# First slots of 128 token-expert pairs for every expert, gathered ahead, and the first batch's scores ahead of the third batch's work

## The chip, the cores and the metric

The kernel runs as one program on one core of a Trainium2 chip. The metric is the device time of one execution in microseconds (us), as the median of several runs; lower is better. Profiles come from one further execution on the same kind of core. PE is the matmul engine, DVE the vector engine, ACT the scalar engine, POOL the general-purpose engine that also issues the indirect DMAs (gathers and scatters by a list of row numbers), SP the engine that issues most plain DMAs.

## What is computed

Two layers on x of shape (8, 256, 512), float32: 2048 tokens, 16 tiles of 128. The reference, cut to what matters here:

```python
def _L0_cond_ref(x, Wq, Wk, Wv, Wo, ..., k_blocks, v_blocks, block_tables, kv_lens):
    ...                       # projections, RMS norm, rotation, paged K/V cache
    p = softmax(where(allowed, qg @ k_all.T * SCALE, -inf))   # window of 256 keys
    return (p @ v_all) @ Wo.T

def _L0_ffn_ref(x, gate_w, W, atoms, expert_atom_weights, importance, mask_idx):
    logits = clip(xt @ gate_w.T, -50, 50)
    top_w, top_idx = top_k(logits, 2);  rw = softmax(top_w)
    weighted = (softmax(expert_atom_weights) @ atoms) * sigmoid(importance)
    ...                       # out = xt @ W.T + sum over 2 experts of
    return out                # rw * (sparse change of W by expert) applied to xt

def _L1_cond_ref(x, W, A, Bm, scalings, adapter_idx):
    return x @ W.T + (x @ A[idx].T @ Bm[idx].T) * scalings[idx]     # per batch

def _L1_ffn_ref(x, gate_w, fc1_w, fc1_b, fc2_w, fc2_b, alpha):
    probs = softmax(x @ gate_w);  gate_score, gate_idx = top_k(probs, 2)
    h = gelu(x @ fc1_w[e] + fc1_b[e]);  y = h @ fc2_w[e] + fc2_b[e]
    return sum over the 2 experts of gate_score/sum * alpha[e] * y

x = x + _L0_ffn_ref(_L0_cond_ref(x, ...), ...)
x = x + _L1_ffn_ref(_L1_cond_ref(x, ...), ...)
```

Each token goes to two of eight experts in each layer, so each layer has 4096 token-expert pairs.

## The kernel before

The work runs in stages, one after the other; the times are those of the profile.

**Projection and keys (0 to about 115 us)** make keys, values and the sparse weight changes, which are added into delta_d in DRAM, one 512x512 weight per expert.

**Attention (115 to 400 us)** takes eight batches in a loop. Batch b first gathers old and new key and value rows for batch b+2 (`find_rows`, `gather_old`, `gather_new`, POOL's indirect DMAs), projects batch b+2's queries on PE (`queries`, L1098) and has DVE normalise and rotate them, and then does `attend` for its own two tiles of 128 tokens: scores ps on PE (L1420), mask and maximum on DVE (L1435), exp on ACT (L1451), sum and scale on DVE, transposes pp (L1465), their copies pT on ACT (L1469), and the product po (L1474), copied to oT (L1484). Between the two tiles `prepared` transposes the keys of batch b+1 (pk L1390, KT L1393). After them `gate_rows` makes the routing logits lg0 of the batch, and `output_rows` (L635) multiplies by Wo and writes rows to h_d in DRAM: tiles 0 to 8 (`EARLY = 9`) inside this loop, the other seven after it. po, pk, pq, pg, pt and the early ph share two PSUM banks under the tag "misc" of the pool ps_o. `start_sums` fills the sums in DRAM from x and zeros.

**Routing of layer 0 (400 to 437 us).** `top2` (cmp L468/L475, sel L482/L483), `shifted_exp` and `normalized` (L498 to L500) choose two experts per token on DVE for all 16 tiles at once, while POOL and ACT re-arrange half of delta (L623). `route` ranks every pair within its expert (`ranks`: pst L215, pn L219, prk L222/L223) and turns ranks into slots by a `Plan`. A *slot* is a group of 128 pairs that is gathered, multiplied and scattered together. `Plan` has two kinds: *full* slots, 128 pairs of one expert fixed in advance, and *paired* slots, two halves of 64 pairs: one half's expert is fixed (`side`), the other's is found at run time (`owner_i`). Layer 0 has 8 full and 26 paired slots, layer 1 has 22 full and 12 paired. `fill_slots` makes the list: one-hot matrices hot (L312) and put (L293 to L305) on DVE, 64 matmul records pm (L319) on PE, giving for each slot 128 row numbers (token_i) and 128 weights (L329). Pairs that find no slot would be handled in a branch (`run_rest`, L1752) that is not entered for these inputs. Between the pm matmuls and beside the last output rows, `fold_adapters` (L1586, L1635, L1646) prepares layer 1's low-rank adapters.

**Slots of layer 0 (437 to 586 us).** For each slot `fetched` (L533) gathers 128 rows of h_d by an indirect DMA, `turned` transposes them (pa L569, copy xsT L575), `multiplied` does the product (full slots L547 with 8 matmuls of 128x512; paired slots L556 with 16 matmuls, each over 64 columns, two abreast), ACT scales by the weight (L1794) and `added` (L580) scatters with addition into one of two sums in DRAM. Gathers run three slots ahead, transposes two. At L1726/L1732, layer 1's fc1 weights (8 MB) and half of fc2 (4 MB) are loaded by SP as soon as their place is free.

**Boundary and layer 1's projection (586 to 684 us).** `fold_gate` (pga L1665) finishes the adapter weights; the two sums are read back (part, L1838) and added to x1; for four groups of four tiles (`quads`; a quad holds one tile of each of four batches) `turn`, `inner` (px L1852) and `outer` (pc L1876, L1887) compute the layer's linear part and adapters; ACT copies each tile to g (L1895) and writes it to g_d (L1896), 16 writes. The order of the quads is not the order of the tiles, and g_d is laid out by tile. The routing of layer 1 runs on DVE and PE beside `outer`. The second half of fc2 is loaded behind the part reads and the writes of x1 to out, fc2's bias (L1937) after the last outer.

**Slots of layer 1 (695 to 968 us).** As in layer 0, with fc1 (pu L1978), gelu (L2004), fc2 (L547 or L556), bias and weight on DVE (L2020, L2021), and the scatter into out (L580).

The order of instructions on each engine is set by a scheduler (with estimates of cost) except where `keep_in_program_order` or `in_a_row` fix it. A gather waits for every write to the DRAM rows that its source names: in both layers the whole of h_d or g_d.

Of the kernel before, what the change touches and what calls it, by code (L numbers as in the profile page):

```python
# [19 lines left out]
P = 128  # L20
# [32 lines left out]
class Plan:  # L53
# [5 lines left out]

    PAIRED, FULL = 128 * HR, 256 * HR  # L60

    def __init__(self, full, side):
        self.full = [e for e in range(E) for _ in range(full[e])]
        self.side = [e for e in range(E) for _ in range(side[e])]
        self.F, self.D = len(self.full), len(self.side)
        self.n = self.F + self.D
        self.by_expert = []
        for e in range(E):
            t = HR * side[e]
            u = t + P * full[e]  # L70
            second = self.PAIRED + HR * (self.F + sum(side[:e]))
            whole = self.FULL + P * sum(full[:e]) - t
            first = HR * self.F - u
            self.by_expert.append((t, u, second + 1, whole - second, first - whole))


PLAN0 = Plan([1] * E, [3] * 6 + [4] * 2)
PLAN1 = Plan([3] * 6 + [2] * 2, [1] * 6 + [3] * 2)
# [3 lines left out]
def two_layer_kernel(ctx: ExitStack, tc: tile.TileContext, io: dict, out: bass.AP):  # L82
# [9 lines left out]
    h_d = dram.tile([N + P, D], F32, name="h_d")  # L92


    g_d = dram.tile([N + P, D], F32, name="g_d")
# [47 lines left out]
    def routing_constants(pool, plan=None, late=False):  # L143
# [36 lines left out]
        nc.gpsimd.iota(tok_i, pattern=[[P, NT]], base=-N, channel_multiplier=1)  # L180
# [7 lines left out]
        if plan:  # L188
            fixed_i = pool.tile([P, 5, E], I32, name="fixed_i")
# [14 lines left out]
            fixed = pool.tile([P, 5, E], F32, name="fixed")  # L204
# [5 lines left out]
    def ranks(pool, psum, consts, sel):  # L210

        earlier, ahead, same_e = consts[:3]
        flat_sel = sel.rearrange("p i e -> p (i e)")
        pst = psum.tile([P, P], F32, name="pst", tag="route_a")
        nc.tensor.transpose(pst, flat_sel, ident)  # L215
        tot = pool.tile([P, 1], F32, name="tot")
        nc.vector.tensor_reduce(tot, pst, AX.X, ALU.add)
        pn = psum.tile([P, E], F32, name="pn", tag="route_a")
        nc.tensor.matmul(pn, tot.to_broadcast([P, P]), same_e, start=True, stop=True)  # L219
        prk = psum.tile([P, NT, E], F32, name="prk", tag="route_b")  # L220
        prk2 = prk.rearrange("p i e -> p (i e)")
        nc.tensor.matmul(prk2, earlier, flat_sel, start=True, stop=False)  # L222
        nc.tensor.matmul(prk2, tot.to_broadcast([P, P]), ahead, start=False, stop=True)  # L223
        return pn, prk
# [21 lines left out]
    def two_rows(pool, rows, cf, row, coef):  # L246
# [4 lines left out]
        at = pool.tile([P, NT, E], F32, name="at")  # L251
        nc.vector.tensor_tensor(
            at, row, rows[:, 1, :, None].to_broadcast([P, NT, E]), ALU.is_equal
# [20 lines left out]
    def fill_slots(keep, pool, psum, tag, consts, slot, rem, cf, n, at_once):  # L274
# [3 lines left out]
        what = pool.tile([P, 2, NT], F32, name="what")  # L278
        nc.vector.tensor_tensor(
            what,  # L280
            tok[:, None, :].to_broadcast([P, 2, NT]),
# [5 lines left out]
        pm = psum.tile([P, 2, n], F32, name="pm", tag="route_b")  # L287
        STEP = 4
        for j in range(0, 2 * NT, STEP):
            if j % at_once == 0:  # L290
                span = slice(j, j + at_once)
                put = pool.tile([P, at_once, 2, n], F32, name="put", tag="wide")
# [18 lines left out]
            hot = pool.tile([P, STEP, P], F32, name="hot", bufs=2)  # L311
# [6 lines left out]
            for k in range(STEP):  # L318
                nc.tensor.matmul(  # L319
                    pm.rearrange("p c s -> p (c s)"),  # L320
                    hot[:, k, :],
                    put[:, (j + k) % at_once].rearrange("p c s -> p (c s)"),
                    start=(j + k == 0),
                    stop=(j + k == 2 * NT - 1),
                )
        token_i = keep.tile([P, n], I32, name=f"token_i_{tag}")
# [3 lines left out]
        return token_i, weight  # L330

    def route(keep, pool, psum, consts, plan, sel, coef, tag, beside=None):
# [8 lines left out]
            boff, boff, float(HR), fixed[:, 4, :], ALU.mult, ALU.add  # L341
# [4 lines left out]
        for j, step in ((0, fixed[:, 3, :]), (1, boff)):  # L346
            past = row if j == 0 else far
            nc.vector.tensor_tensor(
                past, prk, fixed[:, j, None, :].to_broadcast(each), ALU.is_ge
            )  # L350
            nc.vector.tensor_tensor(
                past, past, step[:, None, :].to_broadcast(each), ALU.mult
            )
        nc.vector.tensor_tensor(row, row, far, ALU.add)
# [35 lines left out]
        )  # L390
        owner_i = keep.tile([P, plan.D], I32, name=f"owner_i_{tag}")
        find_owners(pool, owner_i, count, bend)

        if beside:
            beside()
        token_i, weight = fill_slots(
            keep, pool, psum, tag, consts, slot, rem, cf, plan.n, 2 * NT
# [9 lines left out]
        return token_i, weight, owner_i, left_i, (row, rows, left, coef)  # L407

    def route_rest(keep, pool, psum, places, used_i):

        row, rows, left, coef = places
        consts = routing_constants(pool)
# [3 lines left out]
        for r in range(2):  # L416
# [41 lines left out]
        token_i, weight = fill_slots(  # L458
            keep, pool, psum, "rest", consts, slot, rem, cf, NREST, 4
        )  # L460
        return token_i, weight, owner_i

    def top2(pool, val, tag):

        cmp = pool.tile([P, NT, E, E], F32, name=f"cmp_{tag}", tag="wide")
        for o in range(E):
# [3 lines left out]
                other.to_broadcast([P, NT, o + 1]),  # L470
# [3 lines left out]
            if o + 1 < E:  # L474
                nc.vector.tensor_tensor(  # L475
                    cmp[:, :, o + 1 : E, o],
                    other.to_broadcast([P, NT, E - 1 - o]),
                    val[:, :, o + 1 : E],
                    ALU.is_ge,
                )  # L480
        sel = pool.tile([P, NT, E], F32, name=f"sel_{tag}")
        nc.vector.tensor_reduce(sel, cmp, AX.X, ALU.add)  # L482
        nc.vector.tensor_scalar(sel, sel, 1.5, None, ALU.is_lt)  # L483
        return sel

    def shifted_exp(pool, val, tag):
        mx = pool.tile([P, NT], F32, name=f"mx_{tag}")
        nc.vector.tensor_reduce(mx, val, AX.X, ALU.max)
        ex = pool.tile([P, NT, E], F32, name=f"ex_{tag}")
        nc.vector.tensor_tensor(  # L490
            ex, val, mx[:, :, None].to_broadcast([P, NT, E]), ALU.subtract
        )
        nc.scalar.activation(ex, ex, AF.Exp)
        return ex

    def normalized(pool, val, tag):
        sm = pool.tile([P, NT], F32, name=f"sm_{tag}")
# [3 lines left out]
            val, val, sm[:, :, None].to_broadcast([P, NT, E]), ALU.mult  # L501
# [28 lines left out]
    def fetched(pool, rows_d, token_i, s):  # L530
# [6 lines left out]
            in_offset=bass.IndirectOffsetOnAxis(ap=token_i[:, s : s + 1], axis=0),  # L537
            bounds_check=N + P - 1,
# [39 lines left out]
    def added(sum_d, token_i, s, y):  # L578
# [3 lines left out]
            out_offset=bass.IndirectOffsetOnAxis(ap=token_i[:, s : s + 1], axis=0),  # L582
# [14 lines left out]
    delta = [dpool.tile([P, HK, E, D], F32, name="delta_0"), None]  # L597
    ost = ExitStack()
# [32 lines left out]
    def output_rows(i, psum, pool):  # L631

        ph = psum.tile([P, D], F32, name="ph", tag="misc")
# [13 lines left out]
    with ExitStack() as att:  # L647
# [79 lines left out]
        kcos = ap.tile([P, NT, HD], F32, name="kcos")  # L727
        ksin = ap.tile([P, NT, HD], F32, name="ksin")
# [247 lines left out]
        j_i = ap.tile([P, B, NCAND], I32, name="j_i")  # L976
# [21 lines left out]
        code_i = ap.tile([P, B, NCAND], I32, name="code_i")  # L998
# [149 lines left out]
        with proj:  # L1148
# [165 lines left out]
            for i in range(LEAD, NT):  # L1314
# [12 lines left out]
                if i in (6, 8, 10):  # L1327
                    find_rows(i // 2 - 3)
# [41 lines left out]
        sp = att.enter_context(tc.tile_pool(name="sp", bufs=4))  # L1370
        ps_s = att.enter_context(tc.tile_pool(name="ps_s", bufs=2, space=PSUM))
# [158 lines left out]

        beside = iter(())
        for b in range(B):
            kvs = kv_rows[b]
            if b + AHEAD < B:
                if b + AHEAD > 2:
                    find_rows(b + AHEAD)
                gather_old(b + AHEAD)
                gather_new(b + AHEAD)
# [4 lines left out]
            if b + 2 < B:  # L1543
                qrs = queries(b + 2)
# [5 lines left out]
            if b == 1:  # L1550
                for rest in (*sums_d, h_d, g_d):
                    nc.sync.dma_start(rest[N:, :], zero)
            attend(b, 0, kvs, QTs[b], *ready, beside)
            now = ready
# [13 lines left out]
            attend(b, 1, kvs, QTs[b], *now, beside)  # L1568
            gate_rows(b)
# [19 lines left out]
    def fold_adapters(keep, fold, psum):  # L1589
# [8 lines left out]

        an = keep.tile([P, D], F32, name="an")
        bn = fold.tile([P, KC, P], F32, name="bn")  # L1600
        other_side([aT[:, k, :] for k in range(KC)], an, psum)
        other_side(
            [bT[:, k * P : (k + 1) * P] for k in range(KC)], bn.rearrange("p c r -> p (c r)"), psum
        )
# [27 lines left out]
        nc.vector.tensor_scalar(scaled, pick, scal, None, ALU.mult)  # L1632
        for g in range(B // 4):
            pgb = psum.tile([P, D], F32, name="pgb", tag="misc")
# [9 lines left out]
        pbg = psum.tile([P, E], F32, name="pbg", tag="misc")  # L1644
# [46 lines left out]
    rp0 = dst_.enter_context(tc.tile_pool(name="rp0", bufs=1))  # L1691
    with ExitStack() as ffn:
# [435 lines left out]
```

## Time and profile before

| | us |
|---|---|
| Three runs | 976.61, 968.81, 968.16 |
| Median of the runs | 968.81 |
| The profiled execution's own time | 970.09 |
| Its span, from the first to the last instruction | 968.4 |
| PE busy in it | 901.9 |
| DVE busy in it | 455.5 |
| ACT busy in it | 371.8 |
| POOL busy in it | 360.3 |
| Last output row matmul of layer 0 ends | 426.8 |
| First slot gather of layer 0 issued, first slot transpose | 437.0, 442.3 |
| Last matmul of layer 1's projection ends | 684.1 |
| First slot gather of layer 1 issued, first slot transpose | 687.7, 695.3 |

The mean granted clock of PE is 0.979 of full speed. A row of the timeline gives the start, the duration, the engine (ACTq, SPq: an engine's queue issuing a DMA), the source line, the operation, what it writes and reads, its shape and type, a count where several in a row are put together, and in brackets the engine's idle time before it and what ended that. In a list of waits the numbers are the total, the times and the longest.

### The profile page before, as it was taken

The page shows a single profiled execution, that of the slowest core. Times are in us where ns is not written, and L with a number is a line of the kernel's source. Part 1 is how long each engine was busy: PE and PEld are TensorE (multiplying, and loading weights), DVE is VectorE, ACT ScalarE, POOL GpSimd, SP SyncE. Part 2 cuts the span into 40 slices and gives each one's busy share as a digit, 9 for nine tenths or more (in the row PEclk, how much of TensorE's full clock was granted, in tenths as well). Part 3 has the DMA queues.
Part 4 walks back from the last instruction along what each step waited for, and adds up shares of the span by engine and source line. Part 5 has one row for each costly group of instructions (what it writes and reads, how often), then busy time and mean ns, then how long its engine had stood idle before and what let it go on. Part 6 is the DMA issues. An engine that isn't in the chain of part 4 may idle for free. (4 is left out here: it accounts for less than half of the span.)

```text
span 968.4 us, 14307 instructions
## 1 busy us (share of the span) xinstructions
PE 901.9 (93%) x4829; PEld 491.8 (51%) x4829; DVE 455.5 (47%) x1487; ACT 371.8 (38%) x954; POOL 360.3 (37%) x335
## 2 busy tenths in 40 slices
PE   6998889999999997897999997999599999999995
PEld 3554445655555554464433333545377777753332
DVE  5788898846857766672211112470022223223332
ACT  3676475736647599631111113401111111122221
POOL 2721656557564200405666641000233333333211
PEclk9899999999999999997999999999799999999998
DMA  6587692342432212529997768961524443443322
GB/s 194 215 307 269 225 322 45 98 114 60 138 78 61 61 44 66 189 85 326 341 255 133 129 89 222 364 230 54 185 55 76 73 69 66 77 69 63 50 27 34
DMA packets 74237, 134.62 MB, mean 139 GB/s; under 512 B 17309, under 2 KB 22941, under 8 KB 74032
## 3 DMA queue, kind: packets, MB, share of 16 engines
q0 software_dynamic: 25088, 43.68, 24.2%
q1 hardware_dynamic: 38496, 74.57, 22.1%
q10 hardware_dynamic: 10576, 15.39, 4.3%
q8 instruction: 41, 0.67, 0.3%
q14 instruction: 36, 0.29, 0.1%
HBM read 89.95 MB, written 52.56 MB: 147 GB/s over the span
## 5 line engine op out<-in xcount | busy, mean ns | idle before, releaser
L533 POOL DMA_INDIRECT xs<-g_d,token_i_l x34 | 35.2, 1035 | 230.1 <-PE pa L569 129.5
L575 DVE COPY xsT<-pa 128x512 f32<-128x512 f32 x68 | 46.8, 688 | 155.1 <-PE pa L569 146.9
L2020 DVE TENSOR_TENSOR y<-py,b 64x512 f32<-64x512 f32 (+1 forms) x46 | 31.7, 690 | 185.9 <-PE py L547 122.2
L2004 ACT ACTIVATE hs<-pu,b 128x64 f32<-128x64 f32 (+1 forms) x184 | 46.0, 347 | 186.0 <-PE pu L1978 144.5
L1451 ACT ACTIVATE s<-s,mx,roots 128x384 f32<-128x384 f32 x128 | 90.0, 706 | 14.8 <-DVE mx L1447 10.7
L556 PE MATMUL py<-delta,xsT 128*64 128x512 f32 (+1 forms) x416 | 94.8, 598 | 0.0
L1978 PE MATMUL pu<-xsT,w 128*128 128x128 f32 x704 | 83.1, 277 | 0.0
L1978 PEld LDWEIGHTS pu<-xsT,w 128*128 128x128 f32 x704 | 81.1, 194 | 0.4 <-issue 0.4
L547 PE MATMUL py<-w,hs 128*128 128x512 f32 x176 | 79.3, 593 | 0.0
L1474 PE MATMUL po<-pT,kv 128*64 128x128 f32 x768 | 69.4, 285 | 6.4 <-ACT pT L1469 6.4
L580 POOL DMA_INDIRECT out<-y,token_i_l x34 | 53.9, 1584 | 55.8 <-DVE y L2021 51.3
L1159 PE MATMUL pkv<-wkv,xb 128*128 128x512 f32 x128 | 65.4, 635 | 8.3 <-DMA wkv<-wqkvT 8.3
L1131 POOL DMA_INDIRECT delta_d<-entries,put_i x32 | 53.1, 1660 | 53.3 <-DMA delta_d<-entries,put_i 38.6
L1435 DVE CUSTOM_DVE_ANT_0 s<-ps,mask 128x384 f32<-128x384 f32 x128 | 67.2, 550 | 11.3 <-PE ps L1420 11.0
L1794 ACT ACTIVATE y<-py,weight_l 128x512 f32<-128x512 f32 x34 | 23.4, 687 | 125.7 <-PE py L556 87.0
L1474 PEld LDWEIGHTS po<-pT,kv 128*64 128x64 f32 x768 | 47.5, 137 | 43.4 <-ACT pT L1469 30.1
L580 POOL DMA_INDIRECT sums_d<-y,token_i_l x34 | 54.2, 1593 | 31.6 <-ACT y L1794 17.2
L1465 PE MATMUL pp<-ident,s 128*128 128x128 f32 x384 | 60.3, 285 | 4.3 <-DVE s L1462 3.2
L1420 PE MATMUL ps<-KT,QT 64*128 64x384 f32 x256 | 58.1, 533 | 3.5 <-DVE mx L1435 3.5
L1469 ACT COPY pT<-pp 128x384 f32<-128x384 f32 x128 | 55.8, 477 | 9.9 <-PE pp L1465 8.5
L569 PE MATMUL pa<-ident,xs 128*128 128x128 f32 x272 | 43.9, 287 | 16.8 <-DMA xs<-g_d,token_i_l 11.2
L569 PEld LDWEIGHTS pa<-ident,xs 128*128 128x128 f32 x272 | 32.7, 145 | 52.8 <-issue 46.3
(387 smaller groups left out, 1516.3 us busy)
## 6 DMA issues: line engine op xcount, KB each, us to landing
delta_d<-spread SPq DMA_DIRECT2D x16, 512.0 KB
raw<-delta_d SPq DMA_DIRECT2D x16, 512.0 KB
w<-fc_w SPq DMA_DIRECT2D x8, 1024.0 KB
w<-fc_w SPq DMA_DIRECT2D x16, 512.0 KB
part<-sums_d SPq DMA_DIRECT2D x32, 256.0 KB
xb<-xT SPq DMA_DIRECT2D x5, 1024.0 KB
sums_d<-zero SPq DMA_DIRECT2D x18, 256.0 KB
kv_new<-kvt ACTq DMA_DIRECT2D x16, 256.0 KB
```

Of the source, the lines that this page charges most:

```text
L547: nc.tensor.matmul(py, xT[:, k, :], of_expert(experts[0])(weights(k)), start=(k == 0), stop=(k == KC - 1),)
L556: lambda k=k, h=h: nc.tensor.matmul(py[h * HR : (h + 1) * HR, :], xT[:, k, h * HR : (h + 1) * HR], of_expert(experts[h])(weights(k)), star ...
L569: nc.tensor.transpose(dst[:, k, :], src[:, k * P : (k + 1) * P], ident)
L580: nc.gpsimd.indirect_dma_start(out=sum_d, out_offset=bass.IndirectOffsetOnAxis(ap=token_i[:, s : s + 1], axis=0), in_=y, in_offset=None, b ...
L1159: nc.tensor.matmul(pkv, xb[:, k, cols], wkv[:, k, :], start=(k == 0), stop=(k == KC - 1),)
L1420: lambda r=r: nc.tensor.matmul(pss[r], QT[r * HD : (r + 1) * HD, m, t * P : (t + 1) * P], KT[r * HD : (r + 1) * HD, u, t * P : t * P + WU] ...
L1435: nc.vector.tensor_tensor_reduce(out=s, in0=pss[r], in1=mask[:, t, :], scale=1.0, scalar=NEG, op0=ALU.add, op1=ALU.max, accum_out=mx[:, r ...
L1451: nc.scalar.activation(ss[r], ss[r], AF.Exp, bias=mx[:, r : r + 1], scale=root[:, r : r + 1], accum_out=sm[:, r : r + 1],)
L1465: nc.tensor.transpose(pp[:, c * P : (c + 1) * P], s[:, c * P : (c + 1) * P], ident)
L1469: nc.scalar.copy(pT, pp)
L1474: lambda c=c, r=r: nc.tensor.matmul(po[r * HD : (r + 1) * HD, :], kvs[t + c][:, v0 + r * HD : v0 + (r + 1) * HD], pTs[r][:, c * P : (c + 1 ...
L1978: nc.tensor.matmul(pu[:, c, :], w1[:, k, plan.full[s], c * P : (c + 1) * P], xsT[:, k, :], start=(k == 0), stop=(k == KC - 1),)
```

## The change

1. `Plan` gets, for each expert, a first full slot that takes the expert's first 128 pairs in the order of the tiles, and the full slots are ordered with these eight first. They take pairs from the first `tiles` tiles alone: 8 of 16 in layer 0, 12 of 16 (in quad order) in layer 1. A pair of a later tile whose rank is still below 128 is put out of the plan's slots. Layer 0 becomes 16 full and 18 paired slots (34 as before); layer 1 keeps 22 and 12.
2. In layer 0 the lists of these eight slots are found during attention: after batch 4's second `attend`, `choose` selects the experts of tiles 0 to 7 (batches 0 to 3), and `find_first`/`route_early` rank them and make the lists in steps run beside batch 5's `attend`. The sums (pm, 32 columns, four column tiles abreast) and a transpose pt use the "misc" banks; the one-hot matrices use xq's "xb" buffers. The slots' generator `slots0` is started before the remaining output rows, gathers from `h_d[: 8 * 128]`, and its first four slots are recorded inside `route`, so that routing for the other 26 slots (`skip=E`, two column tiles abreast) stands beside them.
3. In layer 1, g_d is laid out in quad order, the list holds two row numbers (`from_i` for g_d, `token_i` for out), and the first eight slots gather from `g_d[: 12 * 128]`.
4. In batch 0 of attention, `ahead()` (the gathers and queries for batch 2) comes after the first `attend` instead of before it; in the other batches it stays before.
5. `fold_adapters` is split: the loads and small operations are recorded in slot 6 of layer 0, the matmuls after the slots, ahead of `fold_gate`. Layer 1's fc1 weights are loaded one expert per slot from slot 8, the first quarter (not half) of fc2 from slot 16, each held back by a small ACT copy from that slot's y; the other three quarters come where the second half came. Routing constants of layer 0 are made in batch 2. The extra 128 rows of h_d and g_d and their two zero fills go.

The diff, cut to its core:

```diff
-            t = HR * side[e]
-            u = t + P * full[e]
+            t = P + HR * side[e]
+            u = t + P * (full[e] - 1)
+            early = self.FULL + P * e
-PLAN0 = Plan([1] * E, [3] * 6 + [4] * 2)
-PLAN1 = Plan([3] * 6 + [2] * 2, [1] * 6 + [3] * 2)
+PLAN0 = Plan([2] * E, [2] * 6 + [3] * 2, 8)
+PLAN1 = Plan([3] * 6 + [2] * 2, [1] * 6 + [3] * 2, 12)
...
-            hot = pool.tile([P, STEP, P], F32, name="hot", bufs=2)
+            hot = hots(j) if hots else pool.tile([P, STEP, P], F32, name="hot", bufs=2)
...
+                in_a_row(
+                    lambda k=k: nc.tensor.matmul(
+                        pm[k % ways * wide : (k % ways + 1) * wide, :],
+                        put_all[:, (j + k) % at_once, :],
+                        hot[:, k, :],
...
+        of_late = slot.rearrange("p (r i) -> p r i", r=2)[:, :, plan.tiles :]
+        far2 = pool.tile([P, 2, NT - plan.tiles], F32, name="far2")
+        nc.vector.tensor_scalar(far2, of_late, E - 0.5, 128.0, ALU.is_lt, ALU.mult)
+        nc.vector.tensor_tensor(of_late, of_late, far2, ALU.add)
...
+        def find_first():
+            first = slice(0, PLAN0.tiles)
...
+            choose(er, first)
+            found = yield from route_early(
+                dpool, er, ps_o, consts0, sel0[:, first, :], coef0[:, first, :], "e", hots
+            )
+            lists0.append((0, found))
...
-            if b + AHEAD < B:
-                if b + AHEAD > 2:
+            def ahead():
+                if b + AHEAD < B:
                     find_rows(b + AHEAD)
-                gather_old(b + AHEAD)
-                gather_new(b + AHEAD)
+                    gather_old(b + AHEAD)
+                    gather_new(b + AHEAD)
+                return queries(b + 2) if b + 2 < B else None
+            qrs = None if b == 0 else ahead()
...
             attend(b, 0, kvs, QTs[b], *ready, beside)
+            if b == 0:
+                qrs = ahead()
...
             attend(b, 1, kvs, QTs[b], *now, beside)
+            if b == 4:
+                beside = find_first()
+                next(beside)
             gate_rows(b)
...
+            def fetch(s):
+                rows_d = h_d[: plan.tiles * P, :] if plan and s < E else h_d
+                xs[s] = fetched(sx, rows_d, columns(lists, s)[0])
...
+    run0 = slots0(lists0, owner0, 0, PLAN0.n, PLAN0)
+    ps_y0 = next(run0)
...
+        choose(tp, slice(PLAN0.tiles, NT))
+        def beside_routing():
+            for i in range(EARLY + 2, NT):
+                output_rows(i, ps_y0, tp, "py")
+            for _ in range(SOME):
+                next(run0)
...
+    for s in range(SOME, PLAN0.n):
+        y = next(run0)
+        if s == SOME + 2:
+            consts1 = routing_constants(rdy, PLAN1, late=True, quads=True)
+            adapters = load_adapters(rp0, rp0)
+        if 0 <= s - E < E:
+            load_first(s - E, y)
+        elif 0 <= s - 2 * E < E:
+            load_second(0, s - 2 * E, y)
...
+            folding = fold_adapters(rp0, rp0, ps_g, *adapters)
...
-                nc.scalar.dma_start(g_d[i * P : (i + 1) * P, :], g)
+                at = (4 * q + j) * P
+                nc.scalar.dma_start(g_d[at : at + P, :], g)
...
+            def fetch(s):
+                rows_d = g_d[: plan.tiles * P, :] if plan and s < E else g_d
+                xs[s] = fetched(sx, rows_d, columns(lists, s)[0])
```

## The prediction

> **What bounds the kernel now.** I read the page's busy shares and slices first, then PE's waits, then the timeline around each wait.
>
> ```profile
> PE 901.9 (93%) x4829; PEld 491.8 (51%) x4829; DVE 455.5 (47%) x1487; ACT 371.8 (38%) x954; POOL 360.3 (37%) x335
> ...
> PE   6998889999999997897999997999599999999995
> ...
> PEclk9899999999999999997999999999799999999998
> ```
>
> PE is the bound: 902 of 968.4 us, and what it lacks is in a few slices. Those around 435–455 and 680–700 us are also the ones where the granted clock falls to 7. PE's list of waits names the holes:
>
> ```profile
> PE pa L569 <- DMA xs<-g_d,token_i_l: 11.2, 1, 11.2
> ...
> PE pa L569 <- issue: 4.7, 1, 4.7
> PE ps L1420 <- DVE mx L1435: 3.5, 3, 2.4
> ```
>
> L569 is the transpose that begins a slot, so each layer's slot loop is entered late. PE's timeline at the entry of layer 0 (start, duration, instruction, count, idle before):
>
> ```profile
> 410.47 16.47 PE L635 MATMUL ph<-woT,oT 128*128 128x512 f32 x38
> 426.78 1.90 PE L319 MATMUL pm<-put,hot 128*128 128x68 f32 x16
> ...
> 442.30 1.09 PE L569 MATMUL pa<-ident,xs 128*128 128x128 f32 x4 [4.75 <-issue]
> 444.21 1.11 PE L569 MATMUL pa<-ident,xs 128*128 128x128 f32 x4 [0.82 <-DMA xs<-h_d,token_i_l]
> 445.11 5.88 PE L547 MATMUL py<-delta,xsT 128*128 128x512 f32 x8
> ...
> 451.27 3.60 PE L547 MATMUL py<-delta,xsT 128*128 128x512 f32 x8
> ```
>
> Output rows end at 426.8; then PE makes the token list (pm), folds the adapters to fill time, and waits for the gather issued at 436.99. The first product takes 5.88 us, the next 3.60. Layer 1, PE then ACT's and POOL's queues:
>
> ```profile
> 670.05 14.00 PE L1887 MATMUL pc<-wc,x1T 128*128 128x512 f32 x32
> 695.25 1.94 PE L569 MATMUL pa<-ident,xs 128*128 128x128 f32 x8 [11.21 <-DMA xs<-g_d,token_i_l]
> 697.22 4.60 PE L1978 MATMUL pu<-xsT,w 128*128 128x128 f32 x32
> ```
> ```profile
> 684.70 0.33 ACTq L1896 DMA_DIRECT2D g_d<-g  x1
> ```
> ```profile
> 687.65 1.09 POOL L533 DMA_INDIRECT xs<-g_d,token_i_l  x1 [99.38 <-DMA g_d<-g]
> ```
>
> The last of 16 row tiles is written at 684.70, the gather leaves when it has landed, and its rows reach PE at 695.25: 10.55 us from write to transpose.
>
> **The change, part by part.** Negative saves.
>
> *1. Entry of layer 0.* The first eight slots are made from tiles 0–7, found during attention. In the built order their gathers wait on rows written in attention and on the last attention product, so POOL issues the first four near 398, thirty us before PE needs them. PE now goes from the output rows straight to two transposes, four pm matmuls and the first product, and spreads the other pm between the products of slots 0–4. Before: output rows end 426.8; the first product ends at 450.99, which at the steady 3.60 is a start of 447.4. Between them lie 20.6 us. After, the same stretch holds: two transposes, to a product near 427.3 (they take 0.6 each; steady cadence already counts one per slot); the pm sums, now two column tiles side by side (64 records took about 7.6; paired, an estimate of 4.3 from the layer-1 projection's px row, 32 records four abreast in 1.08 beside 0.27 for one alone); pt and pl 0.3 each; rest about 0.5. So 427.3 + 5.5 = 432.8 against 447.4: **−14.6**. About 4.2 of this is the adapters' folding, moved and paid in part 5.
> Clock: the first product's extra is 2.28, and the two transposes' extra (1.09 and 1.11 against the steady 0.60) 1.0: 3.3 us by the rows. The Trainium skill, "TensorE: Matmul & The Clock Gate", Part 1, has the array at half clock after an idle window of about 3.4 us until about 3.4 us of sustained work: 1.7 per entry. The window 440–450 shows a granted clock of 0.51 over all 6.88 busy us, since a second hole interrupts the warm-up. At layer 1 row and rule are close (4.60 against the later 3.74, plus 0.9 in transposes: 1.8). The rule would give −13.0 here; I take the row.
> Eight paired slots become full ones. Cadence of full slots is 474.50−470.63 = 3.87, of paired ones 486.81−482.64 = 4.17: 8×0.30 = **−2.4**.
> What could take it back: slot 8 is the first to use the late list, ready near 453 by the pm schedule; gather and landing as before (5.3) give 458.3 against PE near 460, so about 1.7 us of cover. It stands in POOL's queue ahead of slot 9's gather and the scatters, so being late costs its lateness once. The routing's put tensor must exist at 426.7; before it was done at 425.1, now the selection covers half the tiles (about −2) but seven small operations are added: near 423.7, 3 us of cover. A page speaks against it: "SBUF — State Buffer", Who interferes with whom, has VectorE's second port shared with GpSimd as an exclusive lock for whole instructions. The rows agree in kind: VectorE's sel (L483), coef (L500) and nb_i (L231) take 2.07, 1.49 and 1.90 beside POOL's delta copies, 0.23, 0.29 and 0.16 in layer 1 without them, 4.8 us in all. Four gathers (1.0–1.1 each plus 0.3) now precede the copies, so these end near 416, not 412.8. By the rule each of the four copies (2.0–2.6) could block once, 8.7, hence 3.9 over the rows, 0.9 beyond the cover. I take 0, and keep +0.9. Part 1 in all: −17.0, range −19 to −12.
>
> *2. Entry of layer 1.* g_d is now in quad order and the first eight gathers read only the first twelve tiles; in the built order they wait on the twelfth write, in the place of the one at 669.70. Plus the old 10.55 gives 680.3, before PE's last pc ends at 684.05. The routing's list is done by 660 (four to five added small operations, about 1 us against a put at 645.9 needed at 647.7). So the 11.2 wait goes and the 1.8 of slow clock with it. fc2's second part grows from 4.2 to 6.3 MB behind the row reads, at about 340 GB/s +6 us; it lands near 656 and is first needed near 692. Cover 36 us. Late bias load (issued 687, before as after) is needed near 696. I take **−12.5**, range −13 to −9.
>
> *3. First batch's scores first.* Before:
>
> ```profile
> 115.79 7.13 PE L1098 MATMUL pq<-wq,xb 128*128 128x512 f32 x16 [1.05 <-DVE KT L1393]
> 122.85 1.56 PE L1420 MATMUL ps<-KT,QT 64*128 64x384 f32 x8
> 126.83 0.92 PE L1420 MATMUL ps<-KT,QT 64*128 64x384 f32 x4 [2.42 <-DVE mx L1435]
> ```
>
> VectorE rotates the third batch's queries while scores wait: 2.42+0.24+0.85+0.24 = 3.75 idle. With scores ahead, the queries' 7.1 us of matmuls fill the softmax's latency; the same VectorE work remains and some wait returns. Bounds −4 (all) and +1 (rotation late for batch 2); the row nearest the first end, halved: **−2**. Gathers for batch 2 move behind the first scores in POOL's queue; batch 2 starts two batches (68 us) later and covers that.
>
> *4. Lists found in batches 4–5.* PE gains a transpose, two rank products, sixteen small pm four abreast and pt: 0.8 + about 1.5 = 2.3 on a PE busy 9.7–10 of 10 in 230–300. VectorE gains about 13.5 us (half of the old selection 6, ranks and rows 5, four hot at 0.69), where it is busy 3.05–8.77 of 10: hidden on average, late in the softmax bursts. The sums hold one of the two output-row PSUM banks for about a batch, so po, pk and output rows take turns on the other; no row shows that wait. Below it is 0; above, 14 uses by 0.4 (between an oT copy's 0.26 and a 128x512 copy's 0.58) is +5.6. The 23.6–23.9 busy of 24 says other PE work is ready to fill: I take near the lower end, 0.7, so **+3**, range +2 to +8. The added constants (fifteen POOL fills, 13 small VectorE operations in batch 2) are hidden by batch 2; uncovered 0.5.
>
> *5. Boundary of the layers.* The adapters' folding (4.2 us of PE) now follows the layer-0 slots. There PE was idle for 4.2 (2.16 on wn, 0.67 before px, and 1.4 in three smaller), and px at 603.04 waits for the fourth part read, not for PE. Hidden by that read: **+1**; uncovered +3.
>
> *6. Loads.* w1 and the first quarter of w2 are paced one expert per slot from slot 8: 1 MB in 3.9 us is 270 GB/s, below the 347 that window 440–450 moved. Their small ACT copies lie beside PE. **+0.5**. ACT's wait on y adds nothing, ACT being idle there.
>
> Sum: −17.0 −12.5 −2 +3 +1 +0.5 = −27.0. The profiled span 968.4 becomes 941.4; that execution took 970.1, 1.7 over its span and 1.3 over the runs' median of 968.81. From the median: **941.8**, said as 942.
>
> **Rivals.**
> (a) *Attention pays more.* The pinned bank and VectorE's bursts cost the upper bound of part 4 and the first batch gives nothing: +5 +2: 949. For it: VectorE at 8.8 of 10 in the bursts; against: bank users are spread over 34 us.
> (b) *One entry stays.* Layer 1's gathers are late anyway, by traffic (269 GB/s at 690–700), or slot 8's list is. Then 12.5 or about 12 comes back: 954. Against: 3.7 us cover at layer 1.
> (c) *Slower.* The pinned bank decides. If po can't ping-pong and each of about 14 users in batches 4–5 waits for a copy queued behind the softmax's work, 2.0 us each is +28: all of the 27.7 that remain with PE's own 2.3 alone. From there it decides; at 2.5 us each the time is 976. For it: ACT, which makes most of these copies, is up to 9.2 of 10 busy in the bursts; against: PE's list of waits has none on a copy of po or ph.
> (d) *The change doesn't do what it says*: first gathers wait for the last tile after all, or some pairs overflow into the leftover branch. The built order excludes the first; routing of these inputs leaves every expert at least 128 pairs in the first tiles (168–300 and 355–405) and no pair over.
>
> **How the numbers follow.** Main case 0.62 (range 936–948), (a) 0.16, (b) 0.13, (c) 0.07, (d) 0.02. The range 934–956 leaves out (c), (d) and the edge of (b). A run of this kernel can be told from no change at about 1%. Faster by over 1% (below 959) takes main, (a) and most of (b): 0.87; within 1%: 0.06; slower: 0.07.
>
> **What would show it.** Part 1: no idle before the first transpose near 427, granted clock near 1 in 430–450, sixteen slots at 3.87. Part 2: no wait on DMA before layer 1's first transpose, first gather issued near 672. Part 3: ps right after KT near 116. Part 4: batches 4–5 longer by about 3. Part 5: px again near its part read. Wrong: a new wait of pa on slot 8's rows, of po or ph on the bank in 250–320, or layer 1's gather issued after 684.

## The result and the profile after

The changed kernel takes 965.4 us (median of 12 runs, 961.9 to 968.3), the kernel before 972.4 in the same set (12 runs). The ratio is 0.9919, 95% interval 0.9894 to 0.9944: about 8 us faster, where 27 were predicted, and outside the stated 934 to 956. The profiled execution spans 963.5 us against 968.4. The slices of its page:

```profile
PE   5999899995999998798899999899999999999995
...
PEclk9799999997999999899999999999999999999998
```

The weak slice at 690 us is gone (9, clock 9). But there is a new one, the tenth: PE 5, clock 7, at 217 to 241 us, in the middle of attention. PE's waits (total, times, longest):

```profile
PE pp L1599 <- DVE s L1596: 12.9, 5, 10.1
...
PE pa L692 <- DMA xs<-h_d,from_i_l: 3.3, 1, 3.3
PE pm L366 <- DVE put L341: 3.2, 1, 3.2
```

The 11.2 us on g_d have gone. Three waits stand in their place: 10.1 us on VectorE's s, 3.3 on gathered rows and 3.2 on put. Cut at marks that both kernels have, the spans are (the last column is experiment e9 below; pk is the first key transpose, pg a batch's gate product, px the first adapter product, each taken at its start; output rows, slots and pc, the projection's matmuls, at their ends):

| stretch | before | after | e9 |
|---|---|---|---|
| start to pk | 113.6 | 115.1 | 114.9 |
| pk to the first pg (batch 0) | 40.3 | 38.6 | 39.4 |
| first to last pg (batches 1 to 7) | 244.0 | 263.2 | 250.2 |
| last pg to the last output row | 28.9 | 25.8 | 26.7 |
| output rows to the last product of layer 0's slots | 158.7 | 150.6 | 142.1 |
| boundary, to px | 17.4 | 18.2 | 17.6 |
| px to the last pc | 81.0 | 80.2 | 80.2 |
| last pc to the end | 284.3 | 271.8 | 271.7 |

Batch 2 alone, from the pg of batch 1 to its own, grew from 39.3 to 52.8 us. What stopped VectorE there is on its timeline and POOL's:

```profile
215.97 0.19 DVE L180 TENSOR_SCALAR below_e<-below_e 128x64 f32<-128x64 f32 x1
227.93 0.23 DVE L184 CAST count<-count_i 128x128 f32<-128x128 int32 x1 [11.77 <-POOL count_i L182]
```
```profile
222.81 1.57 POOL L1264 DMA_INDIRECT delta_d<-entries,put_i  x1 [1.77 <-DMA delta_d<-entries,put_i]
223.87 3.83 POOL L1244 TENSOR_TENSOR roots<-rs,minus_half 128x8 f32<-128x8 f32 x2
227.12 0.78 POOL L182 IOTA count_i<- 128x128 int32 x1
```

These are layer 0's routing constants, which the change makes in batch 2. Read the two together: VectorE, whose operations on them are kept in program order, comes at 216 to the conversion of count. Its source is filled by POOL at 227.12. The fill takes 0.78 us but stands behind gathers, scatters that each wait for the one before, and the roots. It could not be made before 214, because `count_i` reuses the buffer of `low_i` (its tag), which VectorE reads until then. The other fills had no such tie: although they are recorded in batch 2, POOL made them at the start of the kernel, 200 us before they were used, and VectorE did not wait for them:

```profile
5.76 0.27 POOL L165 IOTA dif_i<- 128x128 int32 x1
5.96 0.27 POOL L177 IOTA below_i<- 128x64 int32 x1
6.14 0.18 POOL L194 IOTA tok_i<- 128x16 int32 x1
```

VectorE's softmax work for batch 2 queues behind the conversion, and PE behind that. In 224 to 234 us the granted clock is 0.50, so PE pays once more after the wait.

The entry of layer 0, on PE:

```profile
426.28 16.47 PE L768 MATMUL ph<-woT,oT 128*128 128x512 f32 x38
442.59 1.04 PE L692 MATMUL pa<-ident,xs 128*128 128x128 f32 x8
446.80 0.66 PE L366 MATMUL pm<-hot,put 128*64 128x128 f32 x8 [3.17 <-DVE put L341]
447.39 3.69 PE L670 MATMUL py<-delta,xsT 128*128 128x512 f32 x8
```
```profile
482.41 0.98 PE L692 MATMUL pa<-ident,xs 128*128 128x128 f32 x4 [3.31 <-DMA xs<-h_d,from_i_l]
483.18 4.97 PE L670 MATMUL py<-delta,xsT 128*128 128x512 f32 x8
```

The first slots' rows are there (no wait at 442.59), as predicted. Then PE waits for put, and at slot 8, the first of the late list, for rows; that second wait also costs 1.4 + 0.4 us of slow clock (4.97 against 3.60, 0.98 against 0.60). On VectorE and POOL, ahead of put:

```profile
429.51 1.89 DVE L443 SCALAR_TENSOR_TENSOR boff<-boff,fixed 128x8 f32<-128x8 f32 x1
432.16 1.77 DVE L293 TENSOR_SCALAR owner_i_l<-owner 128x18 int32<-128x18 f32 x1
```
```profile
429.33 2.04 POOL L748 COPY delta<-raw 128x1024 f32<-128x1024 f32 x1 [1.40 <-DMA raw<-delta_d]
432.10 1.80 POOL L327 MEMSET put<- 128x2048 f32 x1 [0.72 <-DVE owner L292]
```

An operation of eight elements per row lasts 1.89 us and ends with POOL's copy; the next line's lasts 1.77 beside the memset of put (0.17 in the kernel before, with nothing on POOL beside it). On VectorE and POOL, ahead of slot 8:

```profile
472.55 0.31 DVE L397 TENSOR_SCALAR from_i_l<-token_i_l 128x26 int32<-128x26 int32 x1
```
```profile
472.29 1.56 POOL L703 DMA_INDIRECT sums_d<-y,token_i_e  x1 [7.04 <-DVE weight_l L386]
473.29 0.78 POOL L154 MEMSET earlier<- 128x128 f32 x1
474.62 1.10 POOL L656 DMA_INDIRECT xs<-h_d,from_i_l  x1 [0.55 <-issue]
```

The row numbers that slot 8's gather reads are there at 472.9; POOL has a scatter and a fill in hand, issues the gather at 474.62, and its rows reach PE at 482.41.

The entry of layer 1, PE and POOL:

```profile
691.55 1.04 PE L692 MATMUL pa<-ident,xs 128*128 128x128 f32 x8
692.99 3.81 PE L2165 MATMUL pu<-xsT,w 128*128 128x128 f32 x32 [0.40 <-issue]
```
```profile
680.48 1.08 POOL L656 DMA_INDIRECT xs<-g_d,from_i_l  x1 [84.53 <-issue]
```

The gather leaves 11 us before PE's last pc ends, 3.1 after the twelfth write was issued, and PE goes from the pc matmuls into the slots with 0.40 us idle.

### The profile page after: what moved, and what is told of

Read it like the earlier page. It is cut to its first block, busy times and chain, and to the rows that moved or that the text cites. A ratio compares the mean times of both kernels' runs of the same rounds, so it can differ in the third digit from the quotient of the medians.

```text
span 963.5 us, 14351 instructions
## 1 busy us (share of the span) xinstructions
PE 900.4 (93%) x4804; PEld 493.4 (51%) x4804; DVE 470.0 (49%) x1563; ACT 373.4 (39%) x966; POOL 360.8 (37%) x339
## 5 line engine op out<-in xcount | busy, mean ns | idle before, releaser
L656 POOL DMA_INDIRECT xs<-g_d,from_i_l x34 | 35.1, 1034 | 217.4 <-PE pa L692 131.7
L1599 PE MATMUL pp<-ident,s 128*128 128x128 f32 x384 | 62.5, 289 | 14.1 <-DVE s L1596 12.9
L679 PE MATMUL py<-delta,xsT 128*64 128x512 f32 (+1 forms) x288 | 65.5, 598 | 0.0
L1603 ACT COPY pT<-pp 128x384 f32<-128x384 f32 x128 | 56.0, 476 | 13.0 <-PE pp L1599 12.5
L670 PE MATMUL py<-delta,xsT 128*128 128x512 f32 x128 | 59.9, 608 | 0.0
L1599 PEld LDWEIGHTS pp<-ident,s 128*128 128x128 f32 x384 | 42.7, 145 | 31.0 <-issue 16.2
L2070 PE MATMUL pc<-wc,x1T 128*128 128x512 f32 x128 | 58.5, 596 | 0.0
L1231 PE MATMUL pq<-wq,xb 128*128 128x512 f32 x128 | 57.6, 598 | 0.0
```

The costliest lines, as they stand in the source:

```text
L670: nc.tensor.matmul(py, xT[:, k, :], of_expert(experts[0])(weights(k)), start=(k == 0), stop=(k == KC - 1),)
L679: lambda k=k, h=h: nc.tensor.matmul(py[h * HR : (h + 1) * HR, :], xT[:, k, h * HR : (h + 1) * HR], of_expert(experts[h])(weights(k)), star ...
L1231: nc.tensor.matmul(pq, xcols[:, k, :], wq[:, k, :], start=(k == 0), stop=(k == KC - 1))
L1599: nc.tensor.transpose(pp[:, c * P : (c + 1) * P], s[:, c * P : (c + 1) * P], ident)
L1603: nc.scalar.copy(pT, pp)
L2070: nc.tensor.matmul(pc, x1T[:, k, i * P : (i + 1) * P], wc[:, k, :], start=False, stop=(k == KC - 1),)
```

## Experiments

In each, the ratio is to the kernel before, run beside it on the same chip; e1 to e3 and e7 share one set, e4 to e6 another, e8 and e9 a third. Line numbers in fences are those of the changed kernel unless said otherwise.

**e1: count made first** (the changed kernel).

```diff
+        count_i = pool.tile([P, P], I32, name="count_i", tag="low_i")
+        nc.gpsimd.iota(count_i, pattern=[[1, P]], base=0, channel_multiplier=0)
+        count = pool.tile([P, P], F32, name="count")
+        after(nc.vector.tensor_copy(count, count_i))
         low_i = pool.tile([P, NT * E], I32, name="low_i")
...
-        count_i = pool.tile([P, P], I32, name="count_i", tag="low_i")
-        nc.gpsimd.iota(count_i, pattern=[[1, P]], base=0, channel_multiplier=0)
-        count = pool.tile([P, P], F32, name="count")
-        after(nc.vector.tensor_copy(count, count_i))
```

> The changed kernel, with the four lines that make the count constant moved ahead of low_i, whose buffer count_i reuses. In the changed kernel POOL may write count_i only after VectorE has read low_i, and so POOL's fill stands behind gathers, scatters and the roots in batch 2, while VectorE, in program order, waits 11.8 us for it and PE 10.1. Theory A (the constants' wait is lost time on the path): the wait and the slow clock after it go, about 10.1 + 2 to 3, so 12 to 13 us off the 963.5 span, near 951, ratio to the kernel before 0.978 to 0.983. Rival B (POOL's backlog would stop VectorE or PE a little later anyway, on gathered rows or roots): less than 4 us off, ratio 0.988 to 0.993.

Measured: 951.2 us, ratio 0.9806 (0.9771 to 0.9842), span 948.2. Of the 15.3 us that the span is shorter, 13.8 are batch 2's, which takes 39.0 us; nothing took the wait's place. With `count_i` first in its buffer, POOL fills it at the start with the others:

```profile
5.95 0.27 POOL L167 IOTA count_i<- 128x128 int32 x1
```

Theory A.

**e7: the constants alone, in the kernel before.**

```diff
-        consts = routing_constants(tp, PLAN0)
...
+            if b == 2:
+                consts0 = routing_constants(op, PLAN0, late=True)
             attend(b, 0, kvs, QTs[b], *ready, beside)
```

> The kernel before, with one part of the change alone: layer 0's routing constants made in batch 2 in program order (and four tables placed in the projection's pool, as in the change, to make room). Theory A: a VectorE wait of about 10 us on count_i in 205 to 245 us, PE idle beside it, the time 8 to 13 us longer than before, ratio 1.008 to 1.013. Rival B (the wait in the changed kernel comes from the order of batch 0, which delays POOL's gathers, and not from the constants): no such wait, ratio 0.998 to 1.002.

Measured: 976.2 us, ratio 1.0072 (1.0046 to 1.0099). The wait is there without any other part of the change, if shorter than I had set (line numbers of the kernel before):

```profile
223.08 0.23 DVE L178 CAST count<-count_i 128x128 f32<-128x128 int32 x1 [7.91 <-POOL count_i L176]
```

PE waits 6.9 us on VectorE's KT beside it, and batch 2 takes 47.8 us, 8.5 more. So the constants are the cause: e1 takes the wait away, and e7 makes it without the rest of the change. That its length follows from what stands ahead in POOL's queue is my reading. The median is 6.1 us longer, under the 8 to 13 that I had set, and this trace's span only 4.1: its stretches outside attention came out 3.8 us shorter together.

**e8: the changed kernel with batch 0's old order.** `qrs = ahead()` for every batch, and the call after the first attend removed.

> The changed kernel (its constants as they are), with batch 0's gathers and queries put back ahead of its first scores. It asks whether the constants' wait is longer in the changed kernel (batch 2 takes 13.5 us more, 11.8 of VectorE's wait) than in the kernel before with the constants alone (8.5 and 7.9) by reason of batch 0's order. Theory A (batch 0's order pushes POOL's gathers later, so count_i's fill comes later): batch 2 takes 8 to 9 us more than in the kernel before, VectorE's wait on count_i near 8, and the time is 1 to 3 us shorter than the changed kernel, ratio 0.988 to 0.992. Rival B (the two differ by something else in the schedule): batch 2 as in the changed kernel, +13, and the time 1 to 3 us longer, ratio 0.992 to 0.995.

Measured: 961.2 us, ratio 0.9868 (0.9807 to 0.9928), which holds both answers' values. In the trace batch 2 takes 50.0 us (51.6 to 52.9 in the four kernels with the changed kernel's attention) and VectorE waits 9.9 on count_i: between the 7.9 of e7 and the 11.8. Batch 0's order explains part of the difference; the rest stays open.

**e5: e1 with batch 0's old order.**

> The kernel with count made first, with batch 0's gathers and queries put back ahead of its first scores. Theory A: the order of batch 0 is worth what the queries' fill covers, 2 to 3.75 us, so 2 to 4 us longer than with count first, ratio to the kernel before 0.983 to 0.985; the waits of ps on mx, 3.5 us, are back. What attention then takes beyond the kernel before from the first key transpose to the last gate product is the cost of the lists found in batches 4 and 5: +3 by the prediction. Rival B: the order of batch 0 moves the waits only, under 1 us, ratio 0.980 to 0.982, and the lists cost about 2.

Measured: 952.5 us, ratio 0.9813 (0.9786 to 0.9840), not to be told from e1's 0.9806. In the traces pk to the first pg takes 40.5 us here and 38.7 in e1, a saving of 1.8 by the new order; but in e8, with the old order, it takes 38.9, as good as the changed kernel's 38.6. So what the order is worth stays open. The lists can be read better: batches 3 to 5, which hold them, take 3.8 us more here than before (3.9 in the changed kernel), and all of attention 4.4 more, where I had set 3.

**e2: the second half of delta re-arranged by ACT alone.**

```diff
-        relayout = load_delta(1, lp, (nc.gpsimd.tensor_copy, nc.scalar.copy), 8)
+        relayout = load_delta(1, lp, (nc.scalar.copy,), 8)
```

> The changed kernel, with the second half of delta re-arranged by ACT alone instead of ACT and POOL by turns. Theory A (VectorE's small routing operations are held up by POOL's copies, so put comes 3.2 us late for PE): the long VectorE operations of 2 us between 426 and 441 go except beside the put fill, put is done 6 to 8 us earlier, PE's wait of 3.2 on it goes; eight copies of 2.05 on ACT fit in 26 us with the row copies. 2 to 4 us shorter than the changed kernel, ratio 0.988 to 0.990. Rival B (put is late since the attention's last logits are late, or ACT becomes the late one): the wait stays or moves to the output rows' copies, ratio 0.991 to 0.996.

Measured: 960.6 us, ratio 0.9895 (0.9867 to 0.9923). In its trace the same boff takes 0.17 us, only the operations beside the memset stay long, put is ready and PE has no wait on it: output rows to the first product take 1.4 us instead of 4.6. ACT's own price is 0.7 us of wait between output rows. Theory A in the trace; the interval alone would also allow part of B.

**e3: two slots recorded inside the routing.** `SOME = 4` becomes `SOME = 2`.

> The changed kernel, with two slots instead of four recorded inside the routing, so the late list is finished two slots, 7.7 us, earlier. Theory A (slot 8's rows are late, since its list is made over the products of slots 0 to 4 and its gather then takes 10 us of queue and transfer): PE's wait of 3.3 on the gathered rows and the slow clock behind it (1.8) go, about 5 us shorter than the changed kernel, ratio 0.986 to 0.989. Rival B (the gather is slow by other transfers, which come whenever the list does): the wait stays at 2 or more, ratio 0.990 to 0.993.

Measured: 961.8 us, ratio 0.9913 (0.9881 to 0.9946): the gain that I set does not show in the time. In the trace the wait on rows is gone and the slots of layer 0 take 142.4 us instead of 145.9, though the wait on put is still there (3.5) and this time the first product runs slow after it (5.38 against 3.69). So the cause of slot 8's wait is right, and its price is seen in the stretch, not in the median: in this trace the boundary took 2.5 us of it back.

**e6: these three edits (e1, e2, e3) together.**

> The changed kernel with three edits together: count made first, the second half of delta re-arranged by ACT alone, and two slots instead of four recorded inside layer 0's routing. Theory A (the three waits are independent losses on PE's path): PE's waits on s in batch 2, on put and on slot 8's rows all go; against count first alone 3.3 + 2.4 + about 1.8 of slow clock, so a span near 941, ratio 0.972 to 0.976. Rival B (ACT, with eight more copies beside the output rows, or a new wait further on takes half back): ratio 0.977 to 0.981.

Measured: 947.9 us, ratio 0.9759 (0.9732 to 0.9786), span 946.7. None of the three waits is in PE's list. From the last output row to the end of layer 0's slots it takes 142.1 us, 7.6 less than in e1. But the span that I had set was near 941: attention takes 3.8 us more than in e1, 1.6 of it a new wait at 316 us for ACT's copy h of an output row, and the stretches on either side of it 2.6 more. So the span gains 1.5 us on e1, not about 7. The ratio lies at the edge of theory A's range, and a new wait that takes part back is what rival B named; whether ACT's added copies cause it is not shown. The boundary is 20.9 us, as in e1 to e5 and e8 (20.4 to 21.5), against 17.4 before; the 18.2 of the changed kernel's own profile is the lowest of the kernels with this boundary.

**e4: layer 1's gathers from the whole of g_d** (the changed kernel).

```diff
-                rows_d = g_d[: plan.tiles * P, :] if plan and s < E else g_d
+                rows_d = g_d
```

> The changed kernel, with layer 1's first eight gathers reading the whole of g_d again instead of its first twelve tiles. Theory A (the early gathers are what removes layer 1's entry wait): the first gather is issued after the last write, PE waits about 11 us on it and starts on a slow clock, 12 to 13 us longer than the changed kernel, ratio to the kernel before 1.003 to 1.007. Rival B (the entry was shortened by the order of the full slots or the later fc2 loads): less than 4 us longer, ratio below 0.997.

Measured: 981.5 us, ratio 1.0097 (1.0068 to 1.0126).

```profile
708.56 1.94 PE L692 MATMUL pa<-ident,xs 128*128 128x128 f32 x8 [10.87 <-DMA xs<-g_d,from_i_l]
710.48 5.37 PE L2165 MATMUL pu<-xsT,w 128*128 128x128 f32 x32
```

The entry takes 12.8 us instead of 1.3, and the first pu 1.6 longer: 13.1 together, theory A. The ratio is above the one that I had set, for the spans of the two profiles differ by 19.0; the other 6 are not from here: 2.9 at the boundary, 2.1 in layer 0's slots, 1.7 in the projection and 1.8 in attention, less 2.5, most of it ahead of the first key transpose.

**e9: e6 with the gate's copies wn on ACT.**

```diff
             bank,
-            nc.any.tensor_copy,
+            nc.scalar.copy,
             tag="g",
```

> The kernel with the three mends, with the four copies wn of the gate's folding fixed to ACT, where the scheduler had put the last one on VectorE behind additions that wait for part reads. Theory A (that queueing is what leaves the adapters' folding uncovered at the boundary, 20.9 us against 17.4 before): PE's wait of 2.8 on wn goes, and with it the slow clock in the transposes and the first px (about 2.4), the boundary takes 16 to 18 us, ratio to the kernel before 0.971 to 0.974. Rival B (px waits for the part reads anyway, as before): boundary above 19.5, ratio 0.974 to 0.977.

What e9 mends is seen in e1's trace at the boundary, VectorE, then PE:

```profile
587.18 0.69 DVE L2025 TENSOR_TENSOR part<-part,part 128x512 f32<-128x512 f32 x1 [0.66 <-DMA part<-sums_d]
587.79 0.68 DVE L130 COPY wn<-pw 128x512 f32<-128x512 f32 x1
```
```profile
588.52 1.05 PE L131 MATMUL acc<-wn,gw 128*32 128x512 f32 x4 [2.83 <-DVE wn L130]
590.29 1.11 PE L138 MATMUL pt<-ident,parts 128*128 128x128 f32 x4 [0.71 <-ACT parts L135]
591.78 3.68 PE L2031 MATMUL pt<-ident,part 128*128 128x128 f32 x16 [0.38 <-DVE gwc L139]
```

The copy stands in VectorE's order behind additions that wait for part reads, PE waits for it, and then does sixteen transposes in 3.68 us. Measured for e9: 944.8 us, ratio 0.9698 (0.9651 to 0.9744), span 942.8. PE's wait on wn is gone, the same sixteen transposes take 1.96, and the boundary takes 17.6. Theory A by the trace; the ratios of e6 and e9 alone, whose intervals overlap, would not tell the two apart. This version is faster than both kernels, by 3.0% and, by the ratio of the two ratios, about 2.2%.

## Why the prediction was wrong, step by step

**The step that failed** is the last sentence of part 4: "The added constants (fifteen POOL fills, 13 small VectorE operations in batch 2) are hidden by batch 2; uncovered 0.5." I had summed the work on each engine and not followed the one dependence that goes from VectorE to POOL and back: VectorE reads low_i, POOL refills its buffer as count_i, VectorE waits for that. The fills are not work in batch 2 at all, but one of them, of 0.78 us, was tied to it by its buffer. It cost 13.5 us in batch 2: 10.1 and 0.9 of PE's wait, and about 2.5 of slow clock. e1 takes it away and e7 brings it about by itself; with e1 the time, 951.2 us, lies within the stated range. (The 0.5 is also missing from the sum of −27.0, whose 0.5 is part 6's.)

**Part 1** (−17.0) was right in mechanism and wrong in both covers. From the last output row to the end of the slots it gave −8.1 (158.7 to 150.6); without the two waits, in e6, −16.6. For put I had 3 us of cover and took the held operations at the 4.8 us that the trace of before shows; my estimate by the rule of the Trainium skill ("SBUF — State Buffer", Who interferes with whom) was 8.7. Measured beside the four copies: 1.27, 1.89, 2.04 and 2.01 us for operations of 0.16 to 0.29 otherwise, 6.4 in excess, between the row and the rule; beside the memset of put, which is new and which my sum left out, 1.6 more. That makes 8.0 in all. The trace of before had shown what happened to be caught there, not what could be. But the held operations are only a part of it. Counted from the last gate product, put is ready after 29.7 us, where the prediction had 25.7, and PE comes to it sooner: the output rows end 25.8 us after that product, not 28.9, for two of their matmuls now stand ahead of it and of PE's waits behind it (0.83, 0.48 and 1.20) 0.49 is left.

For slot 8 I had a list at the right place relative to PE (472 against 479), but a gather of 5.3 us from issue to rows; it was issued 1.8 us after its row numbers were there (2.7 after the list's weights), behind a scatter and a fill on POOL, and took 7.8. That makes 3.3 of wait and, in this trace, 1.8 of slow clock.

**Part 2** (−12.5): the last pc to the end went from 284.3 to 271.8, −12.5, and e4 gives 13.1 back. The first gather was issued at 680.5; 672 was written for a projection that begins where it did before, 8.5 us earlier.

**Part 3** (−2): batch 0 is 1.7 shorter, but 1.4 shorter in e8 too, without this part of the change; how much of it is the order's is open. **Part 4**, the lists (+3): batch 5, in which most of them are made, takes 38.3 us against 35.5, +2.8; batches 3 to 5 together +3.9, and +3.8 in e5, where batch 0 is as before. PE's waits on a bank come to 1.2 us (pk on the copy of oT, 0.9 of it in batch 2); rival (c) did not occur, and (a), which put the loss on the bank and VectorE's bursts, had the right stage and the wrong cause.

**Part 5** (+1, uncovered +3): +0.8 in the changed kernel's profile, but +3.0 to +4.2 in e1 to e6 and e8. The cover that I named, the part reads, is real (e9: +0.2); what I missed is that a copy of the folding chain can be placed on VectorE behind the additions that wait for those reads.

**Part 6** (+0.5): no wait of PE beside the paced loads; full slots keep 3.87 us.

So of the 22 us between the predicted span (941.4) and the measured one, the constants make 13.5, slot 8 5.1 and put 3.2. The first key transpose was 1.5 later (it lies between 112.5 and 115.1 in all these profiles), and batches 1, 3, 4, 6 and 7 took 2.9 more together (batch 3 alone 2.4: it takes 39.4 us or more in every kernel with batch 0's new order and at most 37.2 with the old, and batch 4 the other way); the stretch after the last gate product took 3.1 less, which belongs with put's 3.2, and the projection 0.8 less. With the waits mended, e9's span is 942.8. That it comes so near is in part luck: attention takes 5.2 us more in it than before, where −2 and +3 were predicted, and the stretch after the last gate product 2.2 less, where nothing was.

## What to carry to other kernels

Work that is "hidden" on an engine with spare time is hidden only if nothing in it waits: follow every operand of a moved step back to the engine that makes it and to what stands ahead of it in that engine's queue, reused buffers among it. Here VectorE, waiting 11.8 us for a fill of 0.78, passed 10.1 on to PE; making the constant first in its buffer took that away. And where a page gives a bound above what the old trace happens to show (here 8.7 against 4.8, and then 6.4 measured), keep the bound in the sum if the overlap is going to change.

## What the runs showed of the hardware

PE's clock after short waits was not the same each time. After 3.17 us on put (the changed kernel) and 3.15 on slot 8's rows (e2) the next product took 3.69 and 3.60 us; after 3.31 on slot 8's rows (the changed kernel) it took 4.97, after 3.27 and 3.48 on put (e1, e3) 5.38. Waits of 2.83, 0.71 and 0.38 close together (e1's boundary) were followed by half speed too, and of 1.79, 0.71 and 0.38 (the changed kernel's) were not: the same sixteen transposes took 3.68 and 1.97 us.

The clock records of the traces tell when it happens. Each stretch of half clock after the first 100 us, the one at the end left out, lasts 3.41, 6.83, 10.24 or 13.65 us, and in each trace their starts lie whole multiples of 3.41 apart: 223.1, 404.0 and 482.5 in the changed kernel. So the clock is set for windows of 3.41 us on a grid that does not move with the work. Slot 8's wait of 3.31 filled one such window (479.1 to 482.5); put's 3.17 was cut by the boundary at 445.0 into 1.3 and 1.8. With all eleven traces cut on their grids, the 41 windows just ahead of a half-clock stretch hold at least 1.49 us of PE's idle time, and the 2614 others at full clock at most 1.95 (by the modelled ends of matmuls). The Trainium skill ("TensorE: Matmul & The Clock Gate", Part 1) has a window of about 3.4 us that runs freely, which agrees, and asks for an idle window; here about half of one was enough. So a wait near 3 us can cost nothing more or almost 2 us more, by its place on the grid.
